# V projection of two head groups per pass, at 256 columns per matmul, with Strassen sums written in place

## The chip, the cores and the metric

The kernel runs on one core of one Trainium2 chip. The metric is the device time of one execution in microseconds (us), the median of several runs. A separate execution was recorded by the hardware profiler; all views of the profile and the trace come from that one. "Span" is the time from its first to its last recorded instruction.

## The reference

Input is x of shape (4, 512, 1024): 4 batches, 512 positions, 1024 channels, in float32, like all weights.

```python
xn = layernorm(x)                               # over the channels, no scale or shift
q, k, v = xn @ Wq, xn @ Wk, xn @ Wv             # 16 heads of 64
q, k = rotary(q), rotary(k)
s = softmax(causal(q @ k.T) / 8) @ v @ Wo       # attention
r = softmax(xn @ gate_w.T)                      # 8 experts
f = ((xn * (r @ in_channel_scale)) @ sign(weight).T) * (r @ out_channel_scale) + bias
out = x + s * silu(f)
```

## The kernel before, in words

**Stages.** The kernel has two stages. The first (lines 696 to 830) goes over the 4 batches and, in each, over 4 groups of heads: 16 steps k, each a (b, g). A group is two "pairs" i of two heads, so its projections have two times 128 channels. In a step TensorE makes Q, K and V of group k, and between these matmuls come the "pieces" of attention: scores, transposes of the probabilities and products with V, of groups k-1 and k-2. The attention output goes to DRAM (at_d), and the normalized, transposed x too (xn_d). The second stage (from line 837) computes the gated part (ffn), the rest of the last attention, and the output projection (project_out).

**Strassen.** A projection of one group multiplies a 1024x256 block of weights with the 1024x512 transposed batch X. Both are cut in quarters, and 7 products take the place of 8 (Winograd's form). Weight quarters: a11 and a12 are the first pair's channels with the first and second half of the contraction, a21 and a22 the second pair's. The sums S1 = a21 + a22, S2 = S1 - a11, S3 = a11 - a21 and S4 = a12 - S2 (form_w, line 243), and T1 to T4 of X (form_x, line 255) are made on VectorE. Products 1 to 7 are, in the order in which they run: 1 = a11 b11, 2 = a12 b21, 7 = S3 T3, 6 = S2 T2, 5 = S1 T1, 4 = a22 T4, 3 = S4 b22. Each has 4 blocks of contraction of 128. Their results are added into the four quarters of the output with the running sums u2 and u3 ("part" tiles): copies on ScalarE, adds on VectorE, one add on GpSimd.

**Q and K against V.** For Q and K (m = 0, 1) the weights are stationary and 256 positions of X stream past (L304). V is wanted with positions on the partitions, so there X is stationary and the 128 channels of a weight quarter stream (L312): eight calls per product, of 128 columns each. Every call in float32 shows in the trace as two weight loads and two matmuls. Results of two products share a bank of PSUM (halves, line 322); for V four banks are used per group. Q and K then go through the rotary embedding (rotary, line 267), for which a list, turn, holds what is due; V is used as it is.

**What sets the order.** TensorE runs in the program's order. project (line 283) is a generator that yields 84 times per group: after each call for Q and K, after two calls for V. interleave (line 756) spreads these 84 steps evenly between the step's pieces, and then runs what is left of the group. The order on VectorE, ScalarE and GpSimd is the scheduler's, by priority and readiness (written out by hand only during the first batch's start). SP's queue issues loads and stores in order; a load into a slot still in use waits there, and so do those behind it.

**Buffers.** Weights of one (group, m) are 1 MB, in a pool of three slots; the load for the key three further on is issued in the course of a key (slot_after, line 373). S1 to S4 and T1 to T4 have one buffer each. PSUM has a ring of 4 banks (bank, line 153) for projections, transposes and values, and four banks for scores. V has 4 buffers, the attention output at (L491) one. Layer-norm input, the signs' weights and the scale tables share two buffers (xip). make_sign and load_sign (lines 556 and 583) turn the FFN weight into signs, in steps k = 4, 8, 12 and 13.

Of the kernel before, what the change touches and what calls it, by code (L numbers as in the profile page):

```python
# [9 lines left out]
F32 = mybir.dt.float32  # L10
# [13 lines left out]
P = 128  # L24
# [27 lines left out]
def attn_gated_ffn_kernel(  # L52
# [3 lines left out]
    wqkv: bass.AP,  # L56
# [66 lines left out]
    sg = [sgp.tile([P, E], F32R, name=f"sg{n}") for n in range(NC)]  # L123
# [17 lines left out]
    atp = right(name="attn", bufs=1)  # L141
# [3 lines left out]
    tabs = left(name="tables", bufs=1)  # L145
    fp = left(name="forms", bufs=1)
    wp = left(name="w", bufs=3)
    tmp = left(name="tmp", bufs=2)

# [73 lines left out]
    W, Q, K, V = {}, {}, {}, {}  # L223

    def load_w(b, g, m):
        w = wp.tile([P, 2, NC, P], F32, tag="w", name=f"w_{b}_{g}_{m}")
        nc.sync.dma_start(out=w.rearrange("p i c n -> p (i c n)"), in_=wqkv[g, m])
        W[b, g, m] = w
# [6 lines left out]
    def quarters_w(key):  # L235
        w = W[key]
        return w[:, 0, :4, :], w[:, 0, 4:, :], w[:, 1, :4, :], w[:, 1, 4:, :]
# [5 lines left out]
    def form_w(key, n):  # L243
        a11, a12, a21, a22 = quarters_w(key)
        f = fp.tile([P, 4, P], F32, tag=f"S{n}", name="S%d_%d_%d_%d" % (n, *key))
        SF[key, n] = f
        x0, x1, op = {
            1: lambda: (a21, a22, ALU.add),
            2: lambda: (SF[key, 1], a11, ALU.subtract),
            3: lambda: (a11, a21, ALU.subtract),  # L250
            4: lambda: (a12, SF[key, 2], ALU.subtract),
        }[n]()
        nc.vector.tensor_tensor(f, x0, x1, op=op)  # L253

    def form_x(b, n):
        b11, b12, b21, b22 = quarters_x(b)
        f = fp.tile([P, 4, TH], F32, tag=f"T{n}", name=f"T{n}_{b}")
        TF[b, n] = f
        x0, x1 = {
            1: lambda: (b12, b11),  # L260
            2: lambda: (b22, TF[b, 1]),
            3: lambda: (b22, b12),
            4: lambda: (b21, TF[b, 2]),
        }[n]()
        nc.vector.tensor_tensor(f, x0, x1, op=ALU.subtract)
# [14 lines left out]
    groups = [(b, g) for b in range(B) for g in range(NGRP)]  # L280
    keys = [(*bg, m) for bg in groups for m in range(3)]

    def project(b, g):

        for m in range(3):
            key = (b, g, m)
            pos = keys.index(key)
            after = keys[pos + 1] if pos + 1 < len(keys) else None
            slot_after = keys[pos + 3] if pos + 3 < len(keys) else None
            a11, a12, a21, a22 = quarters_w(key)  # L290
            b11, b12, b21, b22 = quarters_x(b)
            un = "%d_%d_%d" % key
            c = []
            for i in range(2):
                if m == 2:

                    V[b, g, i] = qk.tile([P, TPB, P], F32, tag="v", name=f"v_{b}_{g}_{i}")
                    c.append(V[b, g, i].rearrange("p t d -> p (t d)"))
                else:
                    c.append(tmp.tile([P, S], F32, tag="c", name=f"c_{un}_{i}"))  # L300
            def product(ps, wq, xq):
                if m < 2:
                    for k in range(4):
                        nc.tensor.matmul(  # L304
                            ps, lhsT=wq[:, k, :], rhs=xq[:, k, :], start=(k == 0), stop=(k == 3)
                        )
                        yield
                else:

                    for j in range(2):  # L310
                        for k in range(4):
                            nc.tensor.matmul(  # L312
                                ps[:, j * P : (j + 1) * P],
                                lhsT=xq[:, k, j * P : (j + 1) * P],
                                rhs=wq[:, k, :],
                                start=(k == 0),
                                stop=(k == 3),
                            )
                            if k % 2:
                                yield  # L320

            def halves(n):

                ps = bank(f"pj_{un}_{n}")
                return ps, ps[:, :TH], ps[:, TH:]

            def part(n):
                return tmp.tile([P, TH], F32, tag=f"part{n}", name=f"part_{un}_{n}", bufs=1)

            def add(out, ps, x):  # L330
                nc.vector.tensor_tensor(out, ps, x, op=ALU.add)  # L331

            _, p, r = halves(1)
            yield from product(p, a11, b11)
            yield from product(r, a12, b21)
            p1 = part(1)
            nc.scalar.copy(p1, p)
            add(c[0][:, :TH], r, p1)
            if turn:
                rotary(*turn.pop(0))  # L340
            _, p, r = halves(2)
            yield from product(r, SF[key, 3], TF[b, 3])
            if pos == 0:

                bank3 = halves(3)
                yield from product(bank3[2], SF[key, 1], TF[b, 1])
            yield from product(p, SF[key, 2], TF[b, 2])
            u2, u3 = part(2), part(3)
            add(u2, p, p1)
            add(u3, r, u2)  # L350
            if turn:
                rotary(*turn.pop(0))
            if after:
                form_w(after, 3)
            if pos:
                ps, p, r = halves(3)
                yield from product(r, SF[key, 1], TF[b, 1])
            else:
                ps, p, r = bank3
            if after:  # L360
                form_w(after, 1)
                form_w(after, 2)
            yield from product(p, a22, TF[b, 4])
            p5 = part(1)
            nc.scalar.copy(p5, r)  # L365
            nc.gpsimd.tensor_tensor(u2, u2, p5, op=ALU.add)  # L366
            nc.vector.tensor_tensor(
                c[1].rearrange("p (h n) -> p h n", h=2),
                ps.rearrange("p (h n) -> p h n", h=2),
                u3[:, None, :].to_broadcast((P, 2, TH)),  # L370
                op=ALU.add,
            )
            if slot_after:
                load_w(*slot_after)
            _, p, _ = halves(4)
            yield from product(p, SF[key, 4], b22)
            add(c[0][:, TH:], p, u2)
            if after:
                form_w(after, 4)
            if m < 2:  # L380

                turn.extend([((b, g, i), m, c[i]) for i in range(2)])
                if m == 0:
                    rotary(*turn.pop(0))
# [91 lines left out]
    def values(u):  # L476
# [14 lines left out]
        at = atp.tile([P, S], F32, tag="at", name="at_%d_%d_%d" % u)  # L491
# [91 lines left out]
    def make_sign(n):  # L583

        for j in range(2):
            cols = slice(j * HALF, (j + 1) * HALF)
            wj, sj = staged[n][:, cols], sg[n][:, cols]
            tc.keep_in_program_order(nc.vector.tensor_scalar(sj, wj, 0.0, None, op0=ALU.is_lt))
            nc.vector.scalar_tensor_tensor(
                sj, wj, 0.0, sj.bitcast(F32), op0=ALU.is_gt, op1=ALU.subtract  # L590
            )
# [87 lines left out]
    W[0, 0, 0] = wp.tile([P, 2, NC, P], F32, tag="w", name="w_0_0_0")  # L679

    def load_half_w(i):
        nc.sync.dma_start(
            out=W[0, 0, 0][:, i].rearrange("p c n -> p (c n)"), in_=wqkv[0, 0][:, i * E : (i + 1) * E]
        )

    load_x(0, 2)
    load_half_w(0)
    load_x(0, 3)
    load_half_w(1)
    nc.sync.dma_start(out=gw[:, :, :NE], in_=gate_wT.rearrange("(c p) e -> p c e", p=P))  # L690
    for m in (1, 2):
        load_w(0, 0, m)
# [3 lines left out]
    first = project(0, 0)  # L696
    with tc.manual_schedule(engines={DVE, ACT}):
# [3 lines left out]
        for t in range(TPB):  # L701
# [12 lines left out]
            for _ in range((0, 4, 3, 0)[t]):  # L714
                next(first)
        next(first)
# [39 lines left out]
    def interleave(pieces, fill, n_fill):  # L756
        done = 0
        for n, piece in enumerate(pieces):
            piece()
            while done * len(pieces) < (n + 1) * n_fill:  # L760
                next(fill, None)
                done += 1
        for _ in fill:
            pass

    late = None, None
    for k, (b, g) in enumerate(groups):
# [4 lines left out]
        if g == 0:  # L772
            routing = [lambda n=n: router(b, n) for n in range(3)]
            if k == 0:
# [4 lines left out]
                    routing[1],  # L779
                    lambda: split_scales(isc),  # L780
                    routing[2],
                    lambda: split_scales(osc),
# [4 lines left out]
            else:  # L787

                pieces.insert(7, routing[0])
                pieces.insert(10, routing[1])  # L790
                pieces.insert(13, routing[2])
        elif g == 1 and b + 1 < B:
            for t in range(2):
                load_x(b + 1, t)
# [16 lines left out]
        if k in (4, 8, 12, 13):  # L811
            n = {4: 0, 8: 2, 12: 4, 13: 6}[k]
# [12 lines left out]
        fill = project(b, g) if k else first  # L825
        interleave(pieces, fill, 3 * 7 * 4)
        if g == NGRP - 1 and b + 1 < B:
            for n in (3, 1, 2, 4):
                form_x(b + 1, n)
# [329 lines left out]
```

## Time and profile before

| | |
|---|---|
| median of 3 runs | 1180.51 us (1179.93 to 1180.64) |
| the profiled execution's own time | 1179.35 us |
| its span | 1177.6 us |
| TensorE clock granted | 0.999 of full speed |
| instructions | 17904 |
| bytes moved by DMA | 122.04 MB, 104 GB/s on average |

How to read the profile's lines: engines are PE (TensorE matmul), PEld (its weight loads, which overlap the matmuls), DVE (VectorE), ACT (ScalarE), POOL (GpSimd) and SP (the queue of SyncE that issues most DMAs). L304 is line 304 of the code. In a list of groups, "out<-in partitions x elements xcount" is followed by busy time and the mean of one; in a source view, three durations are least/median/most in ns. In a waits view, each line is "engine and line <- what it waited for: us in total, times, longest". In a timeline, the first two numbers are start and length in us, and xN instructions are merged into one line. The end of a matmul is modelled by the profiler, so the distance from one start to the next tells more of its price than its duration.

### The profile page before, as it was taken

The numbers are of one execution on the slowest core, as the hardware profiler recorded it, in microseconds if no ns is written. First come the engines' busy times: TensorE is split into PE (matmuls) and PEld (weight loads), VectorE is DVE, ScalarE is ACT, GpSimd is POOL, SyncE is SP. The second block draws the span as 40 slices with busy tenths as digits, with TensorE's granted clock in tenths as the row PEclk, the third lists the DMA queues.
The fourth block names the chain that finished last, engine by engine and source line by source line (L and its number), as shares of the span: only waits on it lengthen the run. The fifth ranks groups of instructions, "written<-read, shape, count | busy, mean of one in ns | idle before, by whom it ended". The sixth has DMA issues, their size and how long they took to land.

```text
span 1177.6 us, 17904 instructions
## 1 busy us (share of the span) xinstructions
PE 1170.6 (99%) x6760; PEld 893.5 (76%) x6760; DVE 754.0 (64%) x1396; ACT 489.3 (42%) x1131; POOL 535.4 (45%) x597
## 2 busy tenths in 40 slices
PE   9999999999999999999999999999999999999998
PEld 8988888887888888887888888787774556645664
DVE  7877677766767677676768776756856543453343
ACT  2454655345464634446464535445532221222120
POOL 0652635344352644344353534355456445543544
PEclk9999999999999999999999999999999999999999
DMA  9422333322152342214226212210505513431320
GB/s 319 140 72 77 121 117 113 92 78 81 46 161 82 99 135 83 81 46 145 97 82 211 73 69 81 81 51 18 215 14 159 190 62 107 147 114 70 108 72 36
DMA packets 60022, 122.04 MB, mean 104 GB/s; under 512 B 5024, under 2 KB 40608, under 8 KB 53920
## 3 DMA queue, kind: packets, MB, share of 16 engines
q1 hardware_dynamic: 55072, 112.11, 29.5%
q0 software_dynamic: 4576, 8.39, 2.1%
q8 instruction: 53, 0.87, 0.3%
q10 hardware_dynamic: 288, 0.39, 0.1%
q14 instruction: 33, 0.27, 0.1%
HBM read 95.45 MB, written 25.43 MB: 103 GB/s over the span
## 4 chain that ended last, share of the span: by engine, by line
PE 98%; DVE 1%; ACT 0%; issue 0%; POOL 0%; DVEq 0%; ACTq 0%; POOLq 0%
PE pj L304 33%; PE pj L312 17%; PE wo L1000 16%; PE ff L881 10%; PE sc L402 7%; PE pv L484 6%; PE ptp L468 6%; PE xtp L209 1%; PE idle L673 1%; PE lg L506 1%; PE os L656 0%; PE is L628 0%; DVE z_t L1025 0%; DVE nmx L417 0%; ACT p L420 0%
## 5 line engine op out<-in xcount | busy, mean ns | idle before, releaser
L430 POOL TENSOR_SCALAR p<-p,rs 128x128 f32<-128x128 f32 (+3 forms) x256 | 167.4, 667 | 212.9 <-DVE rs L428 194.7
L420 ACT ACTIVATE p<-sc,nmx 128x128 f32<-128x128 f32 (+3 forms) x256 | 132.5, 523 | 150.3 <-DVE nmx L417 147.2
L304 PE MATMUL pj<-T,S 128*128 128x256 f32 x768 | 182.3, 380 | 0.0
L304 PEld LDWEIGHTS pj<-T,S 128*128 128x128 f32 x768 | 140.0, 190 | 17.7 <-issue 1.2
L304 PE MATMUL pj<-X,w 128*128 128x256 f32 x512 | 123.1, 381 | 0.2 <-ACT X L215 0.2
L276 POOL TENSOR_TENSOR sw<-sw,sin_sb 128x512 f32<-128x512 f32 x64 | 84.2, 1315 | 76.3 <-ACT sw L274 72.1
L366 POOL TENSOR_TENSOR part<-part,part 128x256 f32<-128x256 f32 x48 | 35.3, 735 | 182.4 <-ACT part L365 168.4
L474 ACT COPY pT<-ptp 128x512 f32<-128x512 f32 x96 | 56.1, 585 | 138.5 <-PE ptp L468 138.0
L417 DVE TENSOR_REDUCE nmx<-sc 128x2 f32<-128x512 f32 (+3 forms) x128 | 103.6, 819 | 2.6
L881 PE MATMUL ff<-sg,hi 128*128 128x512 f32 x256 | 103.4, 404 | 0.0
L304 PEld LDWEIGHTS pj<-X,w 128*128 128x128 f32 x512 | 92.8, 190 | 12.1 <-issue 1.4
L881 PE MATMUL ff<-sg,lo 128*128 128x512 f32 x256 | 99.9, 390 | 0.0
L468 PE MATMUL ptp<-ident,p 128*128 128x128 f32 x640 | 94.7, 273 | 0.3 <-DVE v L331 0.3
L253 DVE TENSOR_TENSOR S<-w 128x512 f32<-128x512 f32 x96 | 77.4, 806 | 27.4 <-PE pj L304 23.9
L312 PE MATMUL pj<-S,T 128*128 128x128 f32 x768 | 91.6, 277 | 0.0
L468 PEld LDWEIGHTS ptp<-ident,p 128*128 128x128 f32 x640 | 78.9, 141 | 14.7 <-DVE v L331 0.5
L273 ACT ACTIVATE sw<-c 32x512 f32<-32x512 f32 x128 | 80.4, 628 | 21.9 <-DVE c L331 19.9
L312 PEld LDWEIGHTS pj<-S,T 128*128 128x128 f32 x768 | 87.8, 192 | 1.7
L277 POOL TENSOR_TENSOR rot<-rot,sw 128x512 f32<-128x512 f32 x64 | 84.1, 1314 | 4.9
L402 PE MATMUL sc<-rot,rot 64*128 64x384 f32 (+3 forms) x512 | 82.1, 449 | 0.0
L274 ACT ACTIVATE sw<-c 32x512 f32<-32x512 f32 x128 | 80.4, 628 | 1.7
L484 PE MATMUL pv<-pT,v 128*64 128x256 f32 (+3 forms) x512 | 76.0, 439 | 0.0
(140 smaller groups left out, 1989.6 us busy)
## 6 DMA issues: line engine op xcount, KB each, us to landing
w<-in_wqkv SPq DMA_DIRECT2D x47, 1024.0 KB, 5.0
x<-in_x SPq DMA_DIRECT2D x16, 512.0 KB, 3.7
xn_d<-X SPq DMA_DIRECT2D x16, 512.0 KB, 5.1
at_d<-at SPq DMA_DIRECT2D x32, 256.0 KB, 2.3
xp<-xn_d SPq DMA_DIRECT2D x16, 512.0 KB, 4.7
ap<-at_d SPq DMA_DIRECT2D x16, 512.0 KB, 4.4
xr<-in_x SPq DMA_DIRECT2D x16, 512.0 KB, 4.4
wb<-in_wb SPq DMA_DIRECT2D x8, 512.0 KB, 3.6
```

The source lines that it names most:

```text
L276: nc.gpsimd.tensor_tensor(sw, sw, sin_sb, op=ALU.mult)
L277: nc.gpsimd.tensor_tensor(rot, rot, sw, op=ALU.add)
L304: nc.tensor.matmul(ps, lhsT=wq[:, k, :], rhs=xq[:, k, :], start=(k == 0), stop=(k == 3))
L312: nc.tensor.matmul(ps[:, j * P : (j + 1) * P], lhsT=xq[:, k, j * P : (j + 1) * P], rhs=wq[:, k, :], start=(k == 0), stop=(k == 3),)
L402: nc.tensor.matmul(ps[:, h, :], lhsT=Q[u][r : r + D, i * P : (i + 1) * P], rhs=K[u][r : r + D, : (i + 1) * P], start=True, stop=True,)
L417: nc.vector.tensor_reduce(nmx, ps, AX.X, ALU.max, negate=True)
L420: nc.scalar.activation(pt[:, h, :], ps[:, h, :], AF.Exp, bias=nmx[:, h : h + 1], accum_out=ssum[:, h : h + 1],)
L430: nc.gpsimd.tensor_scalar(pt[:, h, :], pt[:, h, :], rs[:, h : h + 1], 1.0, op0=ALU.mult, op1=ALU.mult,)
L468: nc.tensor.transpose(tp[:, k, :], probs(u, i)[:, h, j * P : (j + 1) * P], ident)
L484: nc.tensor.matmul(pv[r : r + D, j * P :], lhsT=V[u][:, j, r : r + D], rhs=PT[u][:, n, o : o + (TPB - j) * P], start=(j == 0), stop=(j == ...
L881: nc.tensor.matmul(acc, lhsT=part[q, i][:, c, :], rhs=sg[4 * k + c // 2][:, (c % 2) * HALF : (c % 2 + 1) * HALF], start=(c == 0 and part i ...
L1000: nc.tensor.matmul(ps, lhsT=lhs[:, k, :], rhs=rhs[:, k, :], start=(k == 0), stop=(k == 3))
```

## The change

Groups are taken in twos. In each batch the keys now run (group 0: Q, K), (group 1: Q, K), V of both, (group 2: Q, K), (group 3: Q, K), V of both. V's pass streams 256 columns per matmul, 128 of each group. The steps, 84 per group, run on from one group to the next, and only the end of a batch runs out what is left.

The diff's core:

```diff
+    keys = [
+        (b, g, m)
+        for b in range(B)
+        for g, m in ((0, 0), (0, 1), (1, 0), (1, 1), (0, 2), (2, 0), (2, 1), (3, 0), (3, 1), (2, 2))
+    ]
...
+    waiting = [(key, i) for key in keys for i in range(2) if key[2] == 2 or i == 0]
+    def load_w():
...
+        key, i = waiting.pop(0)
+        b, g, m = key
+        if m < 2:
+            W[key] = wp.tile([P, 2, NC, P], F32, tag="w", name=f"w_{b}_{g}_{m}")
+            nc.sync.dma_start(out=W[key].rearrange("p i c n -> p (i c n)"), in_=wqk[g, m])
+        else:
+            W[key, i] = wp.tile([P, NC, 2 * P], F32, tag="w", name=f"w_{b}_{g}_{m}_{i}")
...
     def form_w(key, n):
...
+        if n == 1:
+            f = a21
+        elif values_too and n != 3:
+            f = a11 if n == 2 else a21
+        else:
+            cols = 2 * P if n == 3 else P
+            f = fp.tile([P, 4 * cols], F32, tag=f"S{n}", name="S%d_%d_%d_%d" % (n, *key))
...
     def form_x(b, n):
...
+        if n > 1:
+            f = fp.tile([P, 4, TH], F32, tag=f"T{n}", name=f"T{n}_{b}")
+        elif b < B - 1:
+            f = sgp.tile([P, 4, TH], F32, tag="last", name=f"T1_{b}")
+        else:
+            f = b12
```

project_qk is the old project for m < 2, with a call of load_w() after product 4 and without the next key's S2 and S4 where that key is a V. The new V pass:

```diff
+    def project_v(key):
...
+        def product(n, wq, xq):
+            ps = bank(f"pj_{un}_{n}").rearrange("p (t c) -> p t c", t=2)
+            for j in range(2):
+                for k in range(4):
+                    nc.tensor.matmul(
+                        ps[:, j, :],
+                        lhsT=xq[:, k, j * P : (j + 1) * P],
+                        rhs=wq[:, k, :],
+                        start=(k == 0),
+                        stop=(k == 3),
+                    )
+                    yield
+            PS[n] = ps
...
+        u2, u3 = (0, 1), (1, 0)
+        yield from product(1, a11, b11)
+        yield from product(2, a12, b21)
+        p1 = part(1)
+        form_w(key, 2)
+        add((0, 0), 2, lambda n: by_group(p1, n))
+        if turn:
+            rotary(*turn.pop(0))
+        yield from product(7, SF[key, 3], TF[b, 3])
+        if turn:
+            rotary(*turn.pop(0))
+        yield from product(6, SF[key, 2], TF[b, 2])
+        add(u2, 6, lambda n: by_group(p1, n))
+        add(u3, 7, lambda n: quarter(n, *u2))
+        if after:
+            form_w(after, 3)
+        yield from product(5, SF[key, 1], TF[b, 1])
+        p5 = part(5)
+        form_w(key, 4)
+        load_w()
+        add((1, 1), 5, lambda n: quarter(n, *u3))
+        for n in range(2):
+            nc.gpsimd.tensor_tensor(
+                quarter(n, *u2), quarter(n, *u2), by_group(p5, n), op=ALU.add
+            )
+        if after:
+            form_w(after, 1)
+            form_w(after, 2)
+        yield from product(4, a22, TF[b, 4])
+        add((1, 0), 4, lambda n: quarter(n, *u3))
+        yield from product(3, SF[key, 4], b22)
+        add((0, 1), 3, lambda n: quarter(n, *u2))
+        load_w()
+        if after:
+            form_w(after, 4)
```

Here quarter(n, i, h) is a part of the V tile of group g+n and pair i, so u2 and u3 lie in V itself; part(n) copies a whole bank on ScalarE; add is two instructions of VectorE, one per group.

Around it: the V tiles have 6 buffers instead of 4; the attention output is written over V's own tile instead of a tile at; the last sign tile, sg7, shares its place with T1 of the first three batches. The weights come in two arrays, wqk as before and wv by two groups. The other pieces move:

```diff
+                    nothing,
+                    routing[2],
                     lambda: split_scales(isc),
-                    routing[2],
-                    lambda: split_scales(osc),
...
-                pieces.insert(7, routing[0])
+                if b < B - 1:
+                    pieces.insert(7, routing[0])
...
         elif g == 1 and b + 1 < B:
-            for t in range(2):
-                load_x(b + 1, t)
+            pieces.insert(12, lambda: [load_x(b + 1, t) for t in range(2)])
+            if b == 0:
+                pieces.insert(6, lambda: split_scales(osc))
...
-        if k in (4, 8, 12, 13):
-            n = {4: 0, 8: 2, 12: 4, 13: 6}[k]
+        if k in (5, 9, 12, 13):
+            n = {5: 0, 9: 2, 12: 4, 13: 6}[k]
...
-        fill = project(b, g) if k else first
-        interleave(pieces, fill, 3 * 7 * 4)
-        if g == NGRP - 1 and b + 1 < B:
-            for n in (3, 1, 2, 4):
-                form_x(b + 1, n)
+        if k == 11:
+            pieces.append(lambda: router(b + 1, 0))
+        interleave(pieces, fill, 3 * 7 * 4 if k else 3 * 7 * 4 - 8)
+        if g == NGRP - 1:
+            for _ in fill:
+                pass
+            if b + 1 < B:
+                for n in (3, 1, 2, 4):
+                    form_x(b + 1, n)
+                fill = projections(b + 1)
```

## The prediction, made before the change was run

> **What bounds the kernel now.** I read the engine shares and the chain of waits first, to learn whose time sets the end; then the waits of TensorE alone, to learn whether that time is work or waiting; then the timeline around one V projection, to get the price of one matmul of each kind; then the two projection lines by themselves.
>
> ```profile
> span 1177.6 us, 17904 instructions
> ...
> PE 1170.6 (99%) x6760; PEld 893.5 (76%) x6760; DVE 754.0 (64%) x1396; ACT 489.3 (42%) x1131; POOL 535.4 (45%) x597
> ...
> PE 98%; DVE 1%; ACT 0%; issue 0%; POOL 0%; DVEq 0%; ACTq 0%; POOLq 0%
> PE pj L304 33%; PE pj L312 17%; PE wo L1000 16%; PE ff L881 10%; PE sc L402 7%; PE pv L484 6%; PE ptp L468 6%; PE xtp L209 1%; PE idle L673 1%; PE lg L506 1%; PE os L656 0%; PE is L628 0%; DVE z_t L1025 0%; DVE nmx L417 0%; ACT p L420 0%
> ```
>
> The chain is 98% matmul. The V projection (L312) has 17% of it, about 200 us. The waits of TensorE show that this is work:
>
> ```profile
> PE idle L673 <- POOL ident masks.py:199: 1.5, 1, 1.5
> PE ptp L468 <- DVE v L331: 0.3, 1, 0.3
> PE xtp L209 <- DVE x L195: 0.3, 1, 0.3
> PE pj L304 <- ACT X L215: 0.2, 1, 0.2
> PE rt L547 <- DVE rex L543: 0.2, 1, 0.2
> ```
>
> 2.5 us of waiting in all, 1.5 of it before the first matmul. So nothing taken from VectorE, ScalarE, GpSimd or the DMAs can pay; a change pays only by cheaper matmuls, and loses by any wait that it puts before them. The timeline of the first groups gives the price:
>
> ```profile
> 81.46 1.89 PE L304 MATMUL pj<-X,S 128*128 128x256 f32 x8
> 83.19 3.73 PE L312 MATMUL pj<-w,X 128*128 128x128 f32 x32
> 86.76 5.52 PE L312 MATMUL pj<-S,T 128*128 128x128 f32 x48
> ```
>
> The second column runs to the modelled end of the last matmul, so I take off that one's duration (275 ns for 128 columns, 379 for 256, from the source views) and divide by the steps: (5.52 - 0.275)/47 = 111.6 ns from start to start at 128 columns, (1.89 - 0.379)/7 = 215.9 ns at 256. Over all 3584 projection matmuls of the trace, leaving out the starts that come over 40 ns late, the means are 111.65 ns (L312) and 216.08 ns (L304). Last, what the V line does and costs besides:
>
> ```profile
> L312 PEld LDWEIGHTS pj<-S,T x768: 186/192/193, 44.5 to 827.8; 128*128 128x128 f32 x192
> L312 PE MATMUL pj<-S,T x768: 274/275/378, 44.6 to 827.9; 128*128 128x128 f32 x192
> ...
> L312 PEldq EVENT_SEMAPHORE  x19: 51/51/51, 37.1 to 809.3; - x19
> ```
>
> Adding its four operand kinds, L312 has 768 + 512 + 256 + 256 = 1792 matmul records: 16 groups x 7 products x 8 calls, each call two records.
>
> **The change, part by part.**
>
> *V matmuls at 256 columns.* 8 passes x 7 products x 8 calls x 2 records = 896 take the place of 1792. The contraction and the number of multiplications stay. Before: 1792 x 111.65 ns = 200.1 us. After, priced by the nearest row, L304's 256-column matmuls with the same 128x128 weights: 896 x 216.08 ns = 193.6 us. All of it is on the chain: **-6.5 us**. One rule speaks against so much. The Trainium skill (TensorE: Matmul & The Clock Gate, "Back-to-back issue gap") gives a fixed 2.5 ns per matmul beside N/2.4 ns. If each record streams its columns twice, 128 columns would be 256/2.4 + 2.5 = 109.2 ns and 256 would be 215.8; the estimate by that page is then 896 x (2 x 109.2 - 215.8) = 2.3 us. L304 agrees with it within 0.3 ns, and so do the transposes of the probabilities, also 128 columns (109.3 ns a start), but L312 stands at 111.65. The transposes' weight loads show 141 ns, those of L312 192: I read the other 2.4 ns a record as the weight load not quite covered by a 128-column matmul. A 256-column one covers it, since L304 has the same loads at 190 ns and no such surcharge. So I take the row, 6.5, and keep 2.3 as the low end.
>
> *Late starts inside the V passes.* 22 starts of L312 followed by L312 come about 102 ns late; 19 queue entries of the kind EVENT_SEMAPHORE stand on that line, second conditions of one instruction. They are for a weight DMA or a bank. The 16 V loads of 1 MB remain 16 (two per pass, and a22 now lies in another tile than a11), while the products fall from 112 to 56. Between 8 fewer and 4 more: -0.8 to +0.4; I take **-0.3 us**. The 93 ns before each score block in the V passes go with the pieces, whose number stays.
>
> *VectorE.* Adds of a pair of V: before 2 x (5 instructions: four of 128x256 at 0.42 us, one of 128x512 at 0.68) = 4.7 us; after 12 of 128x256, reading two runs of 128 from PSUM. The mask add (L413, two runs of 128 in PSUM) has 0.421 us for that shape: 5.0 us. Weight sums of a pair: before 8 of 128x512 at 0.69 to 0.81, 6.1 us; after four of 128x1024, by the 1.22 to 1.33 us of L265's, 5.1 us. Over 8 passes -5 us of 754, at 64% busy, beside TensorE: nothing. If that cover were gone it would still be a gain.
>
> *ScalarE and GpSimd.* Two 512-column copies (0.585 us, L474) for four of 256 (0.37): the same. GpSimd's two adds of 0.735 us stay two. The Q and K passes bunch: five rotaries in an even group, three in an odd one, instead of four; at 2.63 us of GpSimd each, an even group has 13.2 + 16 x 0.667 + 3 x 0.735 = 26 us in some 52. Hidden. If not: one rotary, 2.6 us, ahead of the probabilities that the next transposes need, in 8 groups.
>
> *Sums in place.* S1 written over a21 needs no free buffer, and its wait for the product that read the old S1 (most of VectorE's 23.9 us behind L304) goes; VectorE isn't late, so 0. S2 over a11 must wait for product 1 and is due before product 6: products 2 and 7 lie between, 2 x 16 x 0.216 = 6.9 us, against 1.3 us of work. S4 over a21 is the close one: it can't start before product 5 is done and product 3 needs it, with product 4 alone between, 3.5 us and the pieces that fall there. How long does a VectorE sum after the same product start late today? From the trace, L367's V add starts 1.17 us (median of 16), at most 2.88, after the end of the product it reads. So S4 is ready 1.17 + 1.33 = 2.5 us after product 5 as a rule (0), and 4.2 us at worst: 0.7 us a pass, 6 us in all. A gain is excluded: the old S4 was formed a key earlier. I take 0, the median's value. Queued behind S4 on VectorE are the adds that free product 5's bank; they come late only if S4 does.
>
> *PSUM banks.* Products 1 and 2, and 7 and 6, shared a bank; now each has its own, seven per two groups instead of eight. But product 7's bank is held through product 6: 16 steps at 52.5/84 = 0.63 us, 10 us, not 5, while three or four attention pieces, most of which want a bank, pass on a ring of four. A piece or product that finds none waits for the four adds after product 6, 4 x 0.42 = 1.7 us: 0 to 13.6 us over 8 passes. The nearest row is TensorE's one wait of that kind now, 0.3 us once; I take **+0.1 us a pass, +0.8**. No gain can come of it.
>
> *Weight loads and SP.* Bytes stay. The second half of V's weights takes the slot that the group's second Q key frees after its product 4. From there it is 4 + 16 steps, 12.5 us, to S3's turn on VectorE, and 30 us to the matmul that needs it; 1 MB lands in 5.0 us. Today's distance is over a key more. Issues queued behind it on SP (at_d, x, xn_d) wait as they do now. Moving x's loads into the group leaves some 13 us before the layer norm, against 3.7 to land. 0; if a load came 10 us late, 2.5 at most, once a pass. Signs, scales and the router move between slots whose TensorE work is the same. T1 of the last batch, over b12, waits for the stores of xn_d (5.1 us), with over 7 us of products before T2's turn: 0.
>
> *Attention output in V's tile* drops the single buffer of at, on which nothing of TensorE waits: 0. Six V buffers cover the four live and two draining.
>
> **Sum.** -6.5 - 0.3 + 0.8 = -6.0 us. On the profiled execution: span 1177.6 -> 1171.6, its time 1179.35 -> 1173.3. The median of the runs lies 1.2 us above that execution, so 1180.5 -> **1174.5 us**.
>
> **The rivals.** A: the sum as above, with its small terms varied, 1172.5 to 1177; chance 0.76. B: no change to speak of, in two ways. Either 256 columns bring the page's 2.3 us only, 1180.5 - 2.3 = 1178.2 (against it: L304's measured spacing), or the S4 chain is late as at worst, 1180.5 - 6.5 + 6 = 1180.0 (against it: the median lag). Chance 0.12. C: slower: the banks. The place is between product 7's start and the adds after product 6; the price 1.7 us a pass, 1180.5 - 6.5 + 13.6 = 1187.6. It makes the kernel slower by more than 0.2% from 1.1 us a pass on. For it: the ring is of four and one is now held twice as long; against it: pieces come 2.6 us apart and VectorE and ScalarE empty a bank in 0.6 to 0.7 us. Chance 0.08. D: also most of the 102 ns holes go, L304's included, 1171 to 1172.5; chance 0.04.
>
> 0.2% (2.4 us) is about what a measurement of this kernel tells from no change. A and D are faster, of B a small part: 0.81; same 0.10; slower 0.09. The range 1171.8 to 1178.0 holds A, most of D and the edge of B.
>
> **What would show it.** L312's successor has 896 records with 128x256 at 216 ns a start and takes 194 us of the chain: right; 220 or more there, or many starts 0.5 us late in passes of V: wrong. If S4 is late, the gap stands before product 3 in every V pass and names VectorE's S; if banks, gaps name VectorE's adds on v, between products 7 and 5. TensorE's waits should stay under 5 us in all. The part after the projections, 340 us, should not move by over 1 us. I'd be wrong above all if the matmuls keep their price and the ring doesn't.

## The result, and the profile after

The changed kernel takes 1177.33 us (median of 10 runs, 1175.85 to 1178.05) against 1180.20 us of before in the same session (10 runs, 1179.58 to 1180.64): ratio 0.9975, 95% interval 0.9965 to 0.9985. The gain is 2.9 us, half of the 6.0 forecast. The time lies in the forecast range, 0.7 us from its edge and outside the 1172.5 to 1177 of rival A.

The page of the changed kernel, to lay beside that of before:

```profile
span 1175.7 us, 16090 instructions
...
PE 1166.3 (99%) x5864; PEld 859.9 (73%) x5864; DVE 754.8 (64%) x1380; ACT 488.0 (42%) x1115; POOL 555.2 (47%) x597
...
PE 96%; DVE 2%; ACT 1%; issue 1%; POOL 0%; DVEq 0%; POOLq 0%; ACTq 0%
```

896 matmuls are gone, TensorE's busy time falls by 4 us only, and the chain is now 96% matmul, not 98: other engines have entered it. The source view of the V line, then two lines of the timeline, show that the matmuls cost what was said:

```profile
L429 PE MATMUL pj<-w,X x416: 379/379/483, 71.5 to 828.5; 128*128 128x256 f32 x139
...
L429 PE MATMUL pj<-w,T x352: 379/379/483, 84.0 to 825.0; 128*128 128x256 f32 x176
...
L429 PE MATMUL pj<-S,T x128: 379/379/483, 80.6 to 807.7; 128*128 128x256 f32 x128
L429 PEldq EVENT_SEMAPHORE  x23: 51/51/51, 67.7 to 816.1; - x23
```

```profile
80.56 3.62 PE L429 MATMUL pj<-S,T 128*128 128x256 f32 x16
...
84.02 10.52 PE L429 MATMUL pj<-w,T 128*128 128x256 f32 x48
```

416 + 352 + 128 = 896 records, (10.52 - 0.379)/47 = 215.8 ns from start to start. The waits of TensorE, 2.5 us before, are now:

```profile
PE sc L517 <- ACT p L535: 1.7, 1, 1.7
PE idle L791 <- POOL ident masks.py:199: 1.5, 1, 1.5
PE ptp L583 <- ACT pT L589: 1.2, 1, 1.2
PE xtp L210 <- DVE x L196: 0.3, 1, 0.3
PE pj L342 <- ACT X L216: 0.2, 1, 0.2
```

The first and the third are new, each once in the whole execution, and neither in a V pass. Adding the distances from each matmul's start to the next, by kind, gives the whole account of the two profiled executions (us):

| matmuls | before | after | difference |
|---|---|---|---|
| V | 204.5 | 197.6 | -6.9 |
| Q and K | 394.2 | 394.5 | +0.3 |
| scores | 78.7 | 80.6 | +1.9 |
| transposes of probabilities | 69.9 | 71.2 | +1.2 |
| warm-up at the start | 7.8 | 9.3 | +1.5 |
| all others | 422.6 | 422.5 | -0.1 |
| sum (span 1177.6 to 1175.7) | | | -1.9 |

("All others" takes in the 1.5 us before the first matmul.) So three rows take back 4.6 us of V's 6.9. The experiments ask what each of them is, and whether V's gain really is one of width. All ran beside the kernel before.

### The profile page after: what moved, and what is told of

Same layout as the page of the kernel before. It is cut to its first block, busy times and chain, and to the rows that moved or that the text cites. A ratio compares the mean times of both kernels' runs of the same rounds, so it can differ in the third digit from the quotient of the medians.

```text
span 1175.7 us, 16090 instructions
## 1 busy us (share of the span) xinstructions
PE 1166.3 (99%) x5864; PEld 859.9 (73%) x5864; DVE 754.8 (64%) x1380; ACT 488.0 (42%) x1115; POOL 555.2 (47%) x597
## 4 chain that ended last, share of the span: by engine, by line
PE 96%; DVE 2%; ACT 1%; issue 1%; POOL 0%; DVEq 0%; POOLq 0%; ACTq 0%
PE pj L342 31%; PE wo L1119 16%; PE pj L429 16%; PE ff L1000 10%; PE sc L517 6%; PE pv L599 6%; PE ptp L583 6%; PE xtp L210 1%; PE idle L791 1%; PE lg L622 1%; ACT p L535 0%; DVE S L296 0%; PE os L774 0%; PE is L746 0%; DVE w L296 0%
## 5 line engine op out<-in xcount | busy, mean ns | idle before, releaser
L342 PE MATMUL pj<-X,w 128*128 128x256 f32 x576 | 138.3, 381 | 0.2 <-ACT X L216 0.2
L342 PE MATMUL pj<-T,S 128*128 128x256 f32 x512 | 123.7, 382 | 0.0
L342 PEld LDWEIGHTS pj<-X,w 128*128 128x128 f32 x576 | 105.1, 190 | 14.4 <-issue 1.8
L342 PE MATMUL pj<-T,w 128*128 128x256 f32 x448 | 107.3, 381 | 0.0
L342 PEld LDWEIGHTS pj<-T,S 128*128 128x128 f32 x512 | 93.2, 190 | 13.6 <-issue 1.4
L429 PE MATMUL pj<-w,X 128*128 128x256 f32 x416 | 97.9, 381 | 0.0
L327 POOL TENSOR_TENSOR rot<-rot,sw 128x512 f32<-128x512 f32 x64 | 93.7, 1464 | 4.7
L342 PEld LDWEIGHTS pj<-T,w 128*128 128x128 f32 x448 | 82.2, 190 | 10.7 <-issue 1.0
L429 PEld LDWEIGHTS pj<-w,X 128*128 128x128 f32 x416 | 76.6, 190 | 10.5 <-issue 1.2
L429 PE MATMUL pj<-w,T 128*128 128x256 f32 x352 | 81.9, 383 | 0.0
```

Of the source, the lines that this page charges most:

```text
L327: nc.gpsimd.tensor_tensor(rot, rot, sw, op=ALU.add)
L342: nc.tensor.matmul(ps, lhsT=wq[:, k, :], rhs=xq[:, k, :], start=(k == 0), stop=(k == 3))
L429: nc.tensor.matmul(ps[:, j, :], lhsT=xq[:, k, j * P : (j + 1) * P], rhs=wq[:, k, :], start=(k == 0), stop=(k == 3),)
```

## The experiments

**The start.** The first run repeats the changed kernel unedited.

> The changed kernel once more, to see how much of its missing gain is scatter. The profile after had TensorE busy with the first 42 warm-up transposes for 7.7 us against 6.2 before, and the first projection matmul came 1.45 us later. Theory (the clock's release falls at another moment in each execution): this profile has another length of that row, anywhere from 6 to 8 us, and the runs spread over some 1.5 to 2 us. Rival (the change itself makes the start later, by its other order of loads): again 7.7 us and first projection matmul at 11.5 us. The waits of the score block at 63 us (1.7 us) and of the last transposes at 831 us (1.2 us) come again in both cases.

1177.06 us (1175.92 to 1177.67). The warm-up's line in the timelines of before, of after and of this run:

```profile
1.54 6.24 PE L673 MATMUL idle<-ident 128*128 128x128 f32 x42 [1.54 <-POOL ident masks.py:199]
```

```profile
1.54 7.72 PE L791 MATMUL idle<-ident 128*128 128x128 f32 x42 [1.54 <-POOL ident masks.py:199]
```

The first transpose of x started at 8.64 us in the repeat, at 9.09 in after, at 7.61 in before. Of the distances between the warm-up transposes, 14 were long (mostly 214 ns, then 109) in before, 28 in after, 24 in the repeat. The two waits came again, 1.7 and 1.2 us. The changed kernel was slow at the start twice, which doesn't yet exclude that the change does it; the 128-column run below has the changed kernel's start and 16 long ones, with the first transpose of x at 7.76 us. The next two runs cut the warm-up, in each kernel:

```diff
-    keep_warm(42)
+    keep_warm(28)
```

> The changed kernel with 28 warm-up transposes at the start instead of 42. Theory: with 42, TensorE is still at them when the first layer norm is done (7.5 us) whenever the clock is released late; with 28 they end by 7.5 us even at the slow rate (28 x 0.214 = 6.0 us after 1.5), so the first transposes of x wait for the layer norm alone: 0.3 to 1.5 us less on average than the changed kernel and a smaller spread. Rival: the clock falls back or is released later for want of work, and the first matmuls run at half rate: 1 to 3 us more.

> The kernel before with 28 warm-up transposes instead of 42. Theory (the late start is the clock's release, and has nothing to do with the change): it gains as the changed kernel did, 0.5 to 1.2 us, 1179 to 1179.5, with the runs closer together. Rival: only the changed kernel suffers from it: no change, 1179.9.

Changed kernel: 1175.83 us, four runs from 1175.53 to 1175.92 and two at 1177.2. Kernel before: 1179.30 (1179.05 to 1179.49), against 1180.28 for the unedited one in that session (1179.37 to 1180.88); ratio 0.9992, interval 0.9984 to 1.0000. Both gain about 1 us, the profile of the changed one starts the transposes of x at 7.47 us, that of before at 7.66, and no projection at half rate follows. So the 1.5 us of the account are the moment at which the warm-up went from 214 to 109 ns in that execution; it isn't part of the change. That this is TensorE's clock is inferred from the halved distance: the profile's granted clock reads 1.00 from 1.6 to 4.6 us in before and in after, while both stand at 214 ns. Between profiles with nearly equal starts (before, and the changed kernel with 28) the span falls from 1177.6 to 1174.2: 3.4 us.

**Width alone.** Each V call is cut into two of 128 columns, all else kept:

```diff
             for j in range(2):
-                for k in range(4):
+                for h in range(2):
+                    for k in range(4):
...
-                        ps[:, j, :],
+                            ps[:, j, h * P : (h + 1) * P],
-                        rhs=wq[:, k, :],
+                            rhs=wq[:, k, h * P : (h + 1) * P],
```

> The changed kernel, but each 256-column V call is cut into two of 128 columns: 1792 records again, everything else of the change kept. If the width of the call gives the gain as in the forecast (row of 256 against 128 columns), this is 6.5 us slower than the changed kernel, about 1183.8 us, so slower than before: the rest of the change would then cost some 3.6 us. If the page's fixed 2.5 ns were right, 2.3 us slower, 1179.6. If the gain came from elsewhere (fewer banks, fewer conditions), the same as the changed kernel.

1183.04 us (1182.21 to 1185.16), ratio to before 1.0029 (1.0018 to 1.0041): 6.0 us over the repeat, and 3 us over the kernel before. V's row in the account is 204.0 us, 6.4 more, so the width gives 6.4 of the row's 6.9 us. The 2.3 us (2.2 without rounding, 896 x 2.5 ns) estimated from the formula of the Trainium skill (TensorE: Matmul & The Clock Gate, "Back-to-back issue gap") are refuted here. The prediction left out what the same section says of that formula: it is the gap of an isolated matmul, and counts too little at small N where weight loads run in the stream. That fits the 111.65 ns measured at 128 columns against its 109.2. All else in the change costs about 3 us.

**The score wait.** scores_1 and scores_3 are the code's names for the two score blocks at the start of step k = 1; scores_3 has two units of four records each. In the changed kernel's timeline (VectorE, ScalarE and TensorE):

```profile
54.20 1.13 PE L517 MATMUL sc<-rot,rot 64*128 64x256 f32 x8
...
55.25 0.68 DVE L296 TENSOR_TENSOR S<-w,S 128x512 f32<-128x512 f32 x1
...
55.84 1.29 DVE L325 SCALAR_TENSOR_TENSOR rot<-c,cos_sb 128x512 f32<-128x512 f32 x2
...
57.05 0.43 DVE L528 TENSOR_TENSOR sc<-sc,mask 128x256 f32<-128x256 f32 x1
...
59.22 0.47 ACT L535 ACTIVATE p<-sc,nmx 128x256 f32<-128x256 f32 x1
...
60.21 1.13 PE L517 MATMUL sc<-rot,rot 64*128 64x512 f32 x4
...
61.95 0.47 ACT L535 ACTIVATE p<-sc,nmx 128x256 f32<-128x256 f32 x1
...
62.41 0.47 ACT L535 ACTIVATE p<-sc,nmx 128x256 f32<-128x256 f32 x1
...
63.02 1.13 PE L517 MATMUL sc<-rot,rot 64*128 64x512 f32 x4 [1.68 <-ACT p L535]
```

scores_1 is done at 55.3 us, but its mask starts at 57.05, behind a weight sum and two rotary multiplications on VectorE; ScalarE meanwhile copies for the rotaries and gets to the exponentials at 59.2 and 61.95. The second unit of scores_3 waits for the last of these. The same place in the kernel before:

```profile
53.60 1.14 PE L402 MATMUL sc<-rot,rot 64*128 64x256 f32 x8
...
54.78 0.43 DVE L413 TENSOR_TENSOR sc<-sc,mask 128x256 f32<-128x256 f32 x1
...
59.21 0.47 ACT L420 ACTIVATE p<-sc,nmx 128x256 f32<-128x256 f32 x1
...
60.90 1.99 PE L402 MATMUL sc<-rot,rot 64*128 64x512 f32 x8
```

Two things differ. There a V pass, which has no rotary, ended the step before: the mask started 1.18 us after the block, not 2.85, and the last exponential ended 6.08 us after it, not 8.68. And scores_3 came 7.30 us after scores_1, not 6.01. The change moves two tasks into the pieces of this step, the split of the output scales and the load of x: 84 steps over 8 pieces leave 11 between the blocks, where 84 over 6 left 14. So of 3.9 us of room that are gone, 2.6 are the queues' and 1.3 the closer block's. I tried first an empty piece between scores_1 and scores_3 of this step:

```diff
+        if k == 1:
+            pieces.insert(1, lambda: None)
```

> The changed kernel with an empty piece between the first two score blocks of step k = 1, so that scores_3 comes some 9 steps (4 us) later. Theory: the 1.7 us wait of the second unit's scores_3 at 61 to 63 us is for a score bank that the exponentials of scores_1 still read, late behind the rotary copies on ScalarE, which bunch in this step; it goes, 1.7 us less than the changed kernel, 1175.6. Rival: the probabilities are late by as much wherever the block stands, and the wait comes later in the step: no change.

1179.13 us (1177.01 to 1179.80): 2 us worse than the repeat, though the scores are back at 78.7 us. Its waits and timeline (TensorE, VectorE) say why:

```profile
PE pj L429 <- DVE w L296: 2.7, 1, 2.7
```

```profile
90.08 1.27 DVE L694 SCALAR_TENSOR_TENSOR osc<-osc,row_kind,scales 128x1024 fp32r<-128x1024 f32 x1
91.28 0.74 DVE L455 TENSOR_TENSOR v<-pj,part 128x256 f32<-128x256 f32 x2
...
92.60 0.67 DVE L296 TENSOR_TENSOR S<-w,S 128x512 f32<-128x512 f32 x1
...
93.20 1.74 DVE L296 TENSOR_TENSOR w<-w 128x1024 f32<-128x1024 f32 x1
...
95.00 5.41 PE L429 MATMUL pj<-w,X 128*128 128x256 f32 x16 [2.68 <-DVE w L296]
```

The last VectorE line is S4: product 5 ended at 88.9 us, and S4 started at 93.2, behind the split of the output scales and V's adds, which the shift had moved against each other. Product 3 waited 2.7 us, and eight of its 16 records then came at about 427 ns instead of 216, another 1.7 us; the granted clock reads 0.51 from 95.7 to 99.2 us, and 1.00 before and after. Next, one rotary's copies went from ScalarE to GpSimd:

```diff
+                if (u, m) == ((0, 1, 0), 0):
+                    nc.gpsimd.tensor_scalar(
+                        sw[d : d + 32, :], c[e : e + 32, :], sc, 1.0, op0=ALU.mult, op1=ALU.mult
+                    )
```

> The changed kernel with the four copies of one rotary embedding, the first Q of group 1 in batch 0, made on GpSimd instead of ScalarE; the order on VectorE is the same. Theory: the 1.7 us wait of scores_3 at 61 us comes from five rotaries in the step before, whose copies fill ScalarE ahead of the exponentials of scores_1 (whose score bank is needed); with one rotary less on ScalarE (2.5 us) it goes: 1.7 us less than the changed kernel, about 1175.4. Rival: the exponentials are late by VectorE's own queue (mask and maximum of the second unit): the wait stays at 1 us or more.

1176.38 us (1175.94 to 1177.00), and the wait is 1.1 us: by its size, the rival's case. But the edit slowed VectorE too:

```profile
53.86 1.14 PE L522 MATMUL sc<-rot,rot 64*128 64x256 f32 x8
...
55.48 2.11 DVE L330 SCALAR_TENSOR_TENSOR rot<-c,cos_sb 128x512 f32<-128x512 f32 x2
57.51 0.42 DVE L533 TENSOR_TENSOR sc<-sc,mask 128x256 f32<-128x256 f32 x1
...
58.74 0.47 ACT L540 ACTIVATE p<-sc,nmx 128x256 f32<-128x256 f32 x1 [1.67 <-DVE nmx L537]
```

The two rotary multiplications take 2.11 us instead of 1.29 while GpSimd makes the copies, and the mask starts 3.65 us after the block, 0.8 later than in the changed kernel. ScalarE now stands idle before the first exponential. So both queues had a part in the wait, and this run doesn't tell how much each. Last, the split of the output scales was moved into the gap:

```diff
-                pieces.insert(6, lambda: split_scales(osc))
+                pieces.insert(1, lambda: split_scales(osc))
```

> The changed kernel with one piece of step k = 1 moved: the split of the output scales (three VectorE instructions, 2.7 us) stands between the first two score blocks instead of in V's pass, so that scores_3 comes 10 steps later and VectorE's queue in V's pass is shorter than in the run with the empty piece. Theory (the wait is for VectorE, which has the two rotary multiplications ahead of scores_1's mask when scores_3 follows 10 steps behind; the empty piece cured it but made S4 late behind the split): neither wait, TensorE's score time 78.7 us as before, 1.7 to 2.0 us less than the changed kernel, 1175.3. Rival: VectorE is simply too full in this step, the wait moves to the scores or to S4 again, at 1 us or more.

1174.62 us (1173.96 to 1175.05), ratio to before 0.9952 (0.9938 to 0.9965): 2.4 us less than the repeat. Scores 78.7 us, no wait for scores and none for S4. The timeline shows what helped:

```profile
53.39 1.13 PE L517 MATMUL sc<-rot,rot 64*128 64x256 f32 x8
...
56.23 0.43 DVE L528 TENSOR_TENSOR sc<-sc,mask 128x256 f32<-128x256 f32 x1
...
63.72 1.99 PE L517 MATMUL sc<-rot,rot 64*128 64x512 f32 x8
```

The mask is as late as in the changed kernel, 2.84 us, but scores_3 comes 10.3 us after scores_1. Distance between the two blocks is what was missing; no run has the rotaries in this place with the old distance of 14 steps.

**The last transposes.** In the changed kernel hi and lo, the two parts into which the gated stage splits its input, lie over S and T sums that are free early, so their splits run before V's last adds (ScalarE, VectorE, TensorE in the timeline after the projections):

```profile
827.99 1.67 ACT L764 CAST hi<-xp 128x512 fp32r<-128x512 f32 x3
...
828.65 0.95 DVE L765 TENSOR_TENSOR lo<-xp,hi 128x512 fp32r<-128x512 f32 x1
...
829.86 0.73 DVE L765 TENSOR_TENSOR lo<-xp,hi 128x512 fp32r<-128x512 f32 x1
...
830.52 0.41 DVE L455 TENSOR_TENSOR v<-pj,v 128x256 f32<-128x256 f32 x1
...
830.73 1.07 ACT L589 COPY pT<-ptp 128x512 f32<-128x512 f32 x2
...
831.37 1.09 PE L583 MATMUL ptp<-ident,p 128*128 128x128 f32 x8 [1.18 <-ACT pT L589]
```

The edit exchanges places, so that hi lies over V's weights:

```diff
-    hl = pool(name="hl", bufs=2)
     vec = pool(name="vec", bufs=1)
     wop = pool(name="wo", bufs=1)
+    hl = pool(name="hl", bufs=2)
```

> The changed kernel with the places of the later pools exchanged, so that the tiles hi and lo of the gated stage lie where V's last weights (with S4 in them) are read to the end of the last pass. Nothing else; on ScalarE and VectorE the splits of hi and lo then stand after the last exponentials and V's last adds, as in the kernel before. Theory: the 1.2 us wait of the last transposes (at 830 us) is for a bank held by V's last adds and by copies that stand behind the splits, which the change let run earlier; it shrinks to the 0.3 us of before, and the time from the last projection to the end from 342.4 to 341.4 us: 1.0 us less than the changed kernel. Rival: V's own last adds (two where one was) are late by themselves: the wait stays.

1175.37 us (1175.09 to 1177.42). The median gained more than the wait can explain, with a favourable start (first transpose of x at 7.78 us) and runs in two groups, so I go by the trace. The wait there:

```profile
PE ptp L583 <- DVE v L455: 0.7, 1, 0.7
```

Both were partly right: 0.5 us were the splits, and the 0.4 us that remain over before's 0.3 name V's own last add, two instructions where one was.

**Together.** The edit with the GpSimd copies, the exchange of places, and 28 transposes:

> The changed kernel with the two edits before and 28 warm-up transposes together. If the three causes are apart from each other: 1.2 + 1.0 + 1.7 us less than the changed kernel, about 1173.2, and TensorE's waits in all under 3 us; the whole gain of the V matmuls would then show against before (with 28 transposes too). Rival: one cure brings the next wait: 1174.5 or more.

1174.83 us (1174.76 to 1174.91): the score wait was still 1.1 us, so the rival's bound held. Then with the moved split in place of the GpSimd copies:

> The same with the late splits of hi and lo and with 28 warm-up transposes. If everything adds: 1174.83 us (the run with all three cures so far) less the 1.1 us that its score wait still had, some 1173.6; TensorE's waits 0.7 us (last transposes) beside the start's. This leaves against before, with 28 transposes too (1179.3), 5.7 us of the 6.9 us that V's matmuls save. Rival: the wait moves: 1174.8 or more.

1173.52 us (1173.31 to 1173.54), ratio 0.9943 (0.9930 to 0.9955) to before: faster than both kernels. TensorE's waits:

```profile
PE idle L791 <- POOL ident masks.py:199: 1.5, 1, 1.5
PE xtp L210 <- DVE x L196: 1.1, 2, 0.8
PE ptp L583 <- DVE v L455: 0.7, 1, 0.7
PE pj L342 <- ACT X L216: 0.2, 1, 0.2
```

Against before with 28 transposes (1179.30, in another session) that is 5.8 us.

## Why the prediction was half right, by its own steps

- *V matmuls, -6.5*: right, and by the row. 896 x (2 x 111.65 - 215.96) = 6.6 us, and 6.4 in the run that undid only the width. By the median alone the result lay nearer to rival B (1178.2) than to 1174.5; only the row and the run that undid the width tell them apart. Why a 128-column record costs 2.4 ns more than the formula stays open: the weight load that isn't quite covered was a reading, and no run changed the load.
- *Late starts, -0.3*: none gone. V has 22 of them after as before (2.2 us), Q and K 36 for 33, which is their +0.3. The reason given, second conditions on a DMA or a bank, isn't borne out: all 22 in before are the second record of a call, inside a product, and none follows one of the 19 queue entries within 8 us. What they are stays open.
- *PSUM banks, +0.8, at worst 13.6*: nothing in V's passes. From product 7's start to the end of the adds that read its bank it is 9.4 to 15.2 us, longer than the 10 said in five passes of eight, and no gap stands there.
- *S4, 0*: right for the changed kernel. Its S4 is done 0.4 to 4.2 us before product 3, in all eight passes. The run with the empty piece shows how thin it is: 2.7 us and a clock at half rate.
- *The rotaries bunch, hidden, 0*: this term failed. The sum looked at GpSimd's busy time in a step, which fitted, and the bunch struck on VectorE and ScalarE, once, where two rotary multiplications stood ahead of a mask and their copies ahead of the exponentials: 1.7 us of waiting (1.9 in the account).
- *The moved tasks, 0*: failed with it. The prediction asked what work the moved loads and splits bring to TensorE, and not that each added piece takes its share of the 84 steps: 11 for 14 between the score blocks, 1.3 us of the 3.9 us of lost room.
- *"The part after the projections should not move by over 1 us"*: it moved by 1.0 (341.35 to 342.36 us). The sums in place freed memory early, and the freed memory let other work run too early; I had looked at that from the loads only.
- *The profiled execution stands for the runs*: its start lay 1.5 us later by chance, so the difference of spans, 1.9 us, understates the change.

In sum: -6.9 + 0.3 + 1.9 + 1.2 = -3.5 us by the trace, 2.9 by the medians. The remaining half microsecond isn't settled. With 28 transposes in both kernels the medians differ by 3.5 us (3.1 with each against before in its own session), so part of it may be the start. Where the wait of 1.7 us is, two of six runs lie 1.3 to 2 us above the others (each in the 28-transpose, the late-split and the 128-column run), and where it is gone or down to 1.1 us there are none in 20 runs (the run with the empty piece aside, which has the longer wait for S4). A clock falling to half rate after that wait in some executions, as seen after 2.7 us, would fit. The granted clock of the runs speaks for it in the 28-transpose run (0.998 in the two slow ones, 1.0 in the other four) but not in the late-split run (0.999 in all six), and no profile caught it.

## What to carry to other kernels

Where TensorE is busy 99% of the time, price a change by the distance between matmul starts in the same kernel, and then ask of every moved side task not whether its engine has time over the step, but what stands behind it in that queue at the tightest place, and how close the next block of matmuls follows there. Memory that comes free earlier is a change of order too: what waited for it will run at once, ahead of work that TensorE needs. Two profiles can differ by over a microsecond in their start alone, so compare them by kind of matmul, not by their spans.

## What the runs showed of the hardware

- A float32 matmul record with its own 128x128 weights came every 111.65 ns at 128 columns and every 216.0 ns at 256: 7.3 ns dearer in two halves, while transposes of 128 columns came every 109 ns.
- After a wait of 2.7 us eight matmuls came at about 427 ns instead of 216, with a granted clock of 0.51 over them; a wait of 1.7 us left no such mark in five profiles.
- Between 14 and 28 of the 42 warm-up transposes came some 214 ns apart, the others 109; it was 28 and 24 in two executions of the same program. The 14 more in after than in before were worth 1.5 us. The granted clock read 1.00 meanwhile.
- Two VectorE multiplications took 2.11 us instead of 1.29 while GpSimd made four copies, in both runs that had them; the cause wasn't tested.
